# Layer 2 of a graph network stack: context in four 32-column groups, denominators from sums that DMAs accumulate

## The chip, the cores and the metric

The kernel runs on one NeuronCore of a Trainium2 chip. Five engines work side by side, each through its own queue in order: TensorE (PE; its weight loads, PEld, overlap its products), VectorE (DVE), ScalarE (ACT), GpSimd (POOL) and SyncE (SP), which here only issues DMAs. POOL can issue DMAs too. The metric is the device time of one execution in microseconds, as the median of several runs; beside it stands one profiled execution, whose trace gives every instruction's start and length.

## The reference, cut to layer 2

32 graphs of 512 nodes with 256 features go through four layers, each ending in `x = layernorm(x + layer(x, adj))`. Layers 0, 1 and 3 are graph attention, layer 2 is a transformer block with a mask from the adjacency matrix, made symmetric:

```python
eye = jnp.eye(N, dtype=bool)[None]
allowed = (adj > 0) | (jnp.swapaxes(adj, 1, 2) > 0) | eye
qkv = x @ Wqkv.T + bqkv
q, k, v = (heads(t) for t in jnp.split(qkv, 3, axis=-1))   # 8 heads of 32
scores = jnp.einsum('bhqd,bhkd->bhqk', q * scale, k)
scores = jnp.where(allowed[:, None], scores, -jnp.inf)
attn = jax.nn.softmax(scores, axis=-1)
ctx = jnp.einsum('bhqk,bhkd->bhqd', attn, v)
attn_out = ctx.transpose(0, 2, 1, 3).reshape(B, N, DIM) @ Wo.T + bo
x = _layernorm(x + attn_out, ln1_g, ln1_b)
ff = jax.nn.relu(x @ W1.T + b1) @ W2.T + b2
x = _layernorm(x + ff, ln2_g, ln2_b)
```

## The kernel before

Nodes lie on the 128 partitions in R = 4 blocks of rows; features make K = 2 blocks of 128. All products are in float32 (scores in a one-pass form of it), and each float32 product shows as two records in the trace. One graph is a Python generator, `graph(b)`, which yields before each stretch of PE work the time at which that stretch is due: `PERIOD * b + PLACES[stage][i]`. `heapq.merge` over the 32 generators then emits the stretches in the order of these due times, and under `tc.manual_schedule` that is PE's order, fixed. Only the order of the numbers counts, not their size. About four graphs are in work at a time, so between two stretches of one graph's attention stand feed-forward products of the graph before, layer 0 and layer 1 products of the next, and so on. The order on DVE, ACT, POOL and SP is chosen at build time by a scheduler, and is fixed as well; semaphores between the engines are added by the framework. An engine that waits for one instruction holds up all that stand behind it in its queue.

Layer 2, by its functions:

- `qkv` makes queries and keys, splits them into a high and a low part, and lays the parts out by 128 small DMAs of SP a graph; it copies the values into `v` with one extra column of ones per head (width `VC` = 33).
- `attention` goes over four pairs of heads (`hp`). For each of four blocks j of keys it takes two score products into PSUM banks `s`, an exponential on ACT into a tile `pr` of two heads (128x1024, four buffers), and for j < 3 one multiply by the mask on DVE; for j = 3 the mask enters the scores as a second product (`shut`). Then the context, `cp`: for each j and each head of the pair one product whose stationary operand is 64 columns of `v` (the head's 32, its ones column, and columns of the next head that aren't used). The two heads of a pair write the two halves of the partitions of one bank. The ones column makes the softmax denominators as row 32 of each half. A copy on ACT takes the bank to `cs`.
- `attended` turns `cs` back to rows by 16 transposes, takes the reciprocals of the denominators, multiplies, transposes again (8) and multiplies with `wo`.
- `feed_forward` follows, with a `layernorm` at both ends and a further one for the stack. `layernorm` runs statistics on DVE, a power of -1/2 on POOL (the line of `op=ALU.pow`), one small step on DVE, and four normalising activations on ACT. Layer 0 and layer 1 use it too, so POOL does six such powers and one for layer 0's heads in each graph.

PSUM's eight banks are split by stage: two for layers 0 and 1, four for layer 2 up to the projection, two for feed forward and layer 3 (`bank`).

Of the kernel before, what the change touches and what calls it, by code (L numbers as in the profile page):

```python
# [9 lines left out]
F32 = mybir.dt.float32  # L10
# [3 lines left out]
AF = mybir.ActivationFunctionType  # L14
# [12 lines left out]
PERIOD = 12054  # L27
PLACES = {
    "edges": [-1440, -1440, -410, 1420],
    "x": [3260],  # L30
    "mask": [16220, 16520, 16600, 17520],
    "layer 0": [
        2410, 3594, 4534, 4534, 5073, 5753, 5753, 5823, 6123, 6123, 6233, 6233, 6603, 6773, 6903,
        7687, 7687, 7777, 8077, 8077, 8157, 8287, 8439, 8439,
    ],
    "layer 1": [11037, 11066, 11277, 11729, 11849, 11879, 12043, 13286, 13554, 14195, 14884],
    "qkv": [17180, 17740, 18270, 18270, 18270, 18990, 19484, 19654, 21635, 21635],
    "attention": [
        20262, 20932, 21922, 21982, 22092, 22092, 22092, 22350, 22350, 23077, 23537, 23537,
        24028, 24208, 24328, 24532, 25064, 25220, 25368, 25943,  # L40
    ],
    "projection": [26801, 26801, 26861, 26911, 27661, 27721, 28721, 29140, 29256, 29848],
    "feed forward": [
        31013, 31120, 32042, 32263, 32263, 32465, 32710, 33771, 33983, 34076, 34284, 34691,
        35070, 35329, 35615, 36103, 36646, 37299,
    ],
    "layer 3": [39714, 39714, 40906, 41226, 41406, 41526, 41526, 42359, 42359, 42379, 42379],
}
STAGES = {"edges": "a", "x": "a", "layer 0": "a", "layer 1": "a", "feed forward": "c", "layer 3": "c"}
ALL = mybir.DependencyInfo(mybir.DependencyClass.Sync, mybir.DependencyReason.DATA)  # L50


# [20 lines left out]
def fast_path(ctx: ExitStack, tc: tile.TileContext, a: dict, out: bass.AP, bad: bass.AP):  # L73
# [20 lines left out]
    HC = HO + 1  # L94
    VC = DH + 1
    ND = R * (H + 2 + H2)
# [4 lines left out]
    def product(what, *args, **kwargs):  # L101
        latest[0] = what(*args, **kwargs).ins.name  # L102
# [6 lines left out]
    def paced(b, name, units):  # L109

        i = 0
        while True:
            stage[0] = STAGES.get(name, "b")
            try:
                next(units)
            except StopIteration as end:
                return end.value
            yield PERIOD * b + PLACES[name][i]
            i += 1
# [15 lines left out]
    nc.gpsimd.memset(hv, 1.0)  # L135
    v = const.tile([P, R, H2 * VC + 2 * DH - VC], F32, name="v")
    nc.gpsimd.memset(v, 1.0)

# [105 lines left out]
    def buf(shape, tag, name, bufs, dtype=F32):  # L244

        return sb.tile(shape, dtype, tag=tag + stage[0], name=name, bufs=bufs)

    def bank(name, dtype=F32):
        shape = [P, 2048 // (2 if dtype == BF16 else 4)]
        n = 4 if stage[0] == "b" else 2  # L250
        return ps.tile(shape, dtype, tag="mm" + stage[0], name=name, bufs=n)

    def part(name):

        return buf([P, N], "part", name, {"a": 7, "b": 6, "c": 5}[stage[0]])

# [228 lines left out]
    def qkv(x):  # L485
# [31 lines left out]
        for r in range(R):  # L517
            yield
            p = bank("vp")
            for k in range(K):  # L520
                product(nc.tensor.matmul,
                    p[:, :D],
                    xt[:, k, r * P : (r + 1) * P],
                    wqkv[:, k, 2 * D :],
                    start=k == 0,
                    stop=k == K - 1,
                )
            nc.scalar.copy(
                v[:, r, : H2 * VC].rearrange("p (h e) -> p h e", h=H2)[:, :, :DH],
                p[:, :D].rearrange("p (h e) -> p h e", h=H2),  # L530
            )

        return qk

    def attention(qk, a2, shut):
        cs = []
        for hp in range(H2 // 2):
            pr = []
            for j in range(R):
                yield  # L540
                t = sb.tile([P, 2, N], F32, tag="pr", name="pr", bufs=4)
                for i in range(2):
                    s = bank("s")
                    product(nc.tensor.matmul,
                    s,
                        qk[hp][:, 1, i, j * P : (j + 1) * P],
                        qk[hp][:, 0, i, :],
                        start=True,
                        stop=j < R - 1,
                    )  # L550
                    if j == R - 1:
                        product(nc.tensor.matmul, s, identb, shut, start=False, stop=True)
                    nc.scalar.activation(t[:, i, :], s, AF.Exp, scale=QSCALE)  # L553
                if j < R - 1:
                    edges = a2[:, j, :].unsqueeze(1).to_broadcast([P, 2, N])
                    nc.vector.tensor_mul(t, t, edges)  # L556
                pr.append(t)

            yield
            cp = bank("cp")  # L560
            for j in range(R):
                for i in range(2):
                    first = (2 * hp + i) * VC
                    product(nc.tensor.matmul,
                    cp[i * 2 * DH : (i + 1) * 2 * DH, :],
                        v[:, j, first : first + 2 * DH],
                        pr[j][:, i, :],
                        start=j == 0,
                        stop=j == R - 1,
                    )  # L570
            t = part("cs")
            nc.scalar.copy(t, cp)
            cs.append(t)
        return cs

    def attended(x, cs, rd):
        ctx_ = []
        for r in range(R):
            yield
            p = bank("ctp")  # L580
            for hp in range(H2 // 2):
                product(nc.tensor.transpose,
                    p[:, hp * P : (hp + 1) * P], cs[hp][:, r * P : (r + 1) * P], ident
                )
            o = p.rearrange("p (h e) -> p h e", h=H2)
            rdr = rd[:, r * H2 : (r + 1) * H2].unsqueeze(2)
            nc.vector.reciprocal(rdr, o[:, :, DH : DH + 1])
            if r % 2 == 0:
                t = part("ctx").rearrange("p (r d) -> p r d", d=D)
            ctx_.append(t[:, r % 2, :])  # L590
            nc.vector.tensor_mul(
                ctx_[r].rearrange("p (h e) -> p h e", h=H2),
                o[:, :, :DH],
                rdr.to_broadcast([P, H2, DH]),
            )
        ct = yield from transposed(ctx_, "ct")

# [109 lines left out]

    def attended_all(b, x, cs, rd):
        if b == 0:
            weights2()  # L710
        return (yield from attended(x, cs, rd))

# [10 lines left out]
    def graph(b):  # L723
# [11 lines left out]
        qk = yield from paced(b, "qkv", qkv_all(b, x))  # L735
        cs = yield from paced(b, "attention", attention(qk, *a2))
        y = yield from paced(b, "projection", attended_all(b, x, cs, rds[2]))
        x = yield from paced(b, "feed forward", feed_forward_all(b, x, y))
# [662 lines left out]
```

## Time and profile before

| | |
|---|---|
| median of 3 runs | 3910.5 us (3907.77 to 3911.43) |
| span of the profiled execution | 3904.6 us |
| PE, PEld busy | 3753.3, 2824.5 us |
| DVE, ACT, POOL busy | 2674.8, 1926.2, 346.9 us |
| DMA | 261.20 MB, mean 67 GB/s |
| context products `cp`, 2048 records | 474.9 us busy, 600 ns each |
| scores `s`, 1024 records | 395.1 us, 481 ns |
| transposes `ctp` of `cs` and of `ctx`, 512 and 256 records | 67.2 and 39.5 us |

Busy time is the union of an engine's instruction times; overlapping products share it, so 2048 records of 600 ns make 474.9 us of busy time. In a row of the groups stand the line, the engine, the operation, the tiles written and read, the shape, the count, then busy time and mean length of one, then the idle time of the engine in front of it with what ended it. L102 is the line of the helper `product`, through which all matrix products are recorded, so they are told apart by their tiles. `128*64` is the size of the part of the array that a product uses.

### The profile page before, as it was taken

The page shows a single profiled execution, that of the slowest core. Times are in us where ns is not written, and L with a number is a line of the kernel's source. Part 1 is how long each engine was busy: PE and PEld are TensorE (multiplying, and loading weights), DVE is VectorE, ACT ScalarE, POOL GpSimd, SP SyncE. Part 2 cuts the span into 40 slices and gives each one's busy share as a digit, 9 for nine tenths or more (in the row PEclk, how much of TensorE's full clock was granted, in tenths as well). Part 3 has the DMA queues.
Part 4 walks back from the last instruction along what each step waited for, and adds up shares of the span by engine and source line. Part 5 has one row for each costly group of instructions (what it writes and reads, how often), then busy time and mean ns, then how long its engine had stood idle before and what let it go on. Part 6 is the DMA issues. An engine that isn't in the chain of part 4 may idle for free.

```text
span 3904.6 us, 53602 instructions
## 1 busy us (share of the span) xinstructions
PE 3753.3 (96%) x19238; PEld 2824.5 (72%) x19238; DVE 2674.8 (69%) x5594; ACT 1926.2 (49%) x4257; POOL 346.9 (9%) x266
## 2 busy tenths in 40 slices
PE   5899999999999999999999999999999999999996
PEld 4577777777777777777777777777777777777764
DVE  4667676677677677677677677677777677777653
ACT  2444455444455544455544455545555544555442
POOL 0000010000010001010001010001010001010000
PEclk6899999999999999999999999999999999999998
DMA  3222222222222222222222222222222222221120
GB/s 106 77 73 65 72 58 67 71 76 67 70 60 65 71 76 69 68 62 63 71 76 71 66 63 64 69 76 71 66 65 65 65 76 74 63 67 58 49 54 12
DMA packets 180431, 261.20 MB, mean 67 GB/s; under 512 B 36800, under 2 KB 72768, under 8 KB 180160
## 3 DMA queue, kind: packets, MB, share of 16 engines
q1 hardware_dynamic: 180160, 257.71, 23.1%
q8 instruction: 155, 2.54, 0.3%
q14 instruction: 116, 0.95, 0.1%
HBM read 106.57 MB, written 16.78 MB: 32 GB/s over the span
## 4 chain that ended last, share of the span: by engine, by line
PE 60%; DVE 14%; issue 8%; ACT 5%; POOL 5%; POOLq 0%; ACTq 0%
PE o L102 16%; PE f1p L102 7%; PE f2p L102 6%; PE qkp L102 5%; PE cp L102 5%; DVE pr L556 4%; ACT y L275 4%; POOL rs L270 3%; PE h3p L102 3%; PE s L102 3%; PE h1p L102 3%; PE wop L102 3%; POOL st L297 2%; PE gp L102 2%; PE vp L102 2%
## 5 line engine op out<-in xcount | busy, mean ns | idle before, releaser
L556 DVE TENSOR_TENSOR pr<-pr,a 128x1024 f32<-128x1024 f32 x384 | 459.1, 1216 | 319.3 <-ACT pr L553 319.2
L275 ACT ACTIVATE y<-y,rs 128x256 f32<-128x256 f32 x768 | 398.4, 589 | 438.2 <-DVE rs L271 438.2
L393 DVE SCALAR_TENSOR_TENSOR pt<-gb,ex,at 128x512 f32<-128x512 f32 x768 | 530.6, 744 | 77.6 <-ACT gb L345 77.6
L553 ACT ACTIVATE pr<-s 128x512 f32<-128x512 f32 x1024 | 545.2, 613 | 7.4 <-PE s L102 7.3
L102 PEld LDWEIGHTS o<-hv,pt 128*128 128x128 f32 x4096 | 508.4, 199 | 23.7 <-issue 8.4
L102 PE MATMUL o<-hv,pt 128*128 128x65 f32 x4096 | 502.7, 280 | 9.7 <-DVE pt L393 9.7
L102 PE MATMUL f2p<-wf,ft 128*128 128x256 f32 x2048 | 491.6, 383 | 12.3 <-ACT ft L638 12.2
L102 PE MATMUL cp<-pr,v 128*64 128x512 f32 x2048 | 474.9, 600 | 17.8 <-DVE pr L556 17.1
L102 PE MATMUL f1p<-yt,wf 128*128 128x256 f32 x2048 | 488.9, 381 | 0.3 <-DVE yt L302 0.3
L102 PE MATMUL o<-h,pt 128*128 128x257 f32 x2048 | 482.8, 383 | 3.7 <-DVE pt L393 3.7
L102 PEld LDWEIGHTS o<-h,pt 128*128 128x128 f32 x2048 | 381.5, 190 | 96.0 <-issue 40.6
L270 POOL TENSOR_TENSOR rs<-rs,mhalf 128x4 f32<-128x4 f32 x192 | 246.2, 1282 | 2118.8 <-DVE rs L269 1826.0
L638 ACT ACTIVATE ft<-f1p,cols 128x256 f32<-128x256 f32 x512 | 215.2, 474 | 442.2 <-PE f1p L102 442.2
L102 PEld LDWEIGHTS f2p<-wf,ft 128*128 128x128 f32 x2048 | 380.1, 191 | 69.5 <-ACT ft L638 17.1
L102 PEld LDWEIGHTS f1p<-yt,wf 128*128 128x128 f32 x2048 | 385.3, 191 | 54.5 <-DVE yt L302 0.8
L102 PE MATMUL s<-qk 128*128 128x512 f32 x1024 | 395.1, 481 | 1.6 <-ACT pr L553 1.6
L102 PEld LDWEIGHTS cp<-pr,v 128*64 128x64 f32 x2048 | 133.0, 136 | 286.0 <-issue 194.2
L266 DVE BATCH_NORM_STATS2 bn<-y 128x6 f32<-128x256 f32 x768 | 294.6, 411 | 4.5
L102 PEld LDWEIGHTS s<-qk 128*128 128x128 f32 x1024 | 187.8, 190 | 99.3 <-issue 40.6
L102 PE MATMUL qkp<-xt,wqkv 128*128 128x512 f32 x512 | 231.3, 594 | 0.0
L345 ACT COPY gb<-gp 128x512 f32<-128x512 f32 x192 | 111.5, 581 | 219.4 <-PE gp L102 219.4
L428 DVE RECIPROCAL rd<-o 128x4 f32<-128x4 f32 x128 | 23.4, 183 | 272.7 <-PE o L102 272.7
(134 smaller groups left out, 4582.5 us busy)
## 6 DMA issues: line engine op xcount, KB each, us to landing
qk<-hi SPq DMA_DIRECT2D x1024, 64.0 KB, 2.0
qk<-lo SPq DMA_DIRECT2D x1024, 64.0 KB, 2.0
adjt<-in_adjt SPq DMA_DIRECT2D x64, 512.0 KB, 3.5
adj<-in_adj SPq DMA_DIRECT2D x64, 512.0 KB, 3.6
xt<-in_xt SPq DMA_DIRECT2D x32, 512.0 KB, 3.4
x<-in_x SPq DMA_DIRECT2D x32, 512.0 KB, 4.7
out<-y SPq DMA_DIRECT2D x32, 512.0 KB, 3.0
wf<-in_w1t SPq DMA_DIRECT2D x1, 1024.0 KB, 7.6
```

The source lines that it names most:

```text
L102: latest[0] = what(*args, **kwargs).ins.name
L266: nc.vector.bn_stats(st[:, r, :], y[:, r, :])
L270: nc.gpsimd.tensor_tensor(rs[:, 1, :], rs[:, 0, :], mhalf[:, :R], op=ALU.pow)
L275: nc.scalar.activation(y[:, r, :], y[:, r, :], AF.Identity, bias=rs[:, 2, r : r + 1], scale=rs[:, 1, r : r + 1],)
L297: nc.gpsimd.tensor_tensor(st[:, 2, :], st[:, 1, :], mhalf[:, :G], op=ALU.pow)
L345: nc.scalar.copy(g, p)
L393: nc.vector.scalar_tensor_tensor(t, g, f, edges, op0=ALU.max, op1=ALU.mult)
L428: nc.vector.reciprocal(rdh, o[:, :, HO:])
L553: nc.scalar.activation(t[:, i, :], s, AF.Exp, scale=QSCALE)
L556: nc.vector.tensor_mul(t, t, edges)
L638: nc.scalar.activation(ft[:, f, :], p[:, f, :], AF.Relu, bias=bf1[:, ff + f : ff + f + 1])
```

## The change

Context: the loop now goes over the two column blocks c of the context. Four heads share one bank, each with its 32 columns of `v` (no ones column any more), so the four products of a block of keys write four groups of 32 partitions. The scores of two head pairs alternate, j by j; the context products come in two blocks per c, after j = 1 and after j = 3. `cp` lies the right way round already: a copy takes it into `ct`.

Denominators: the tiles of j = 1, 2, 3 are added onto that of j = 0 by DMAs that accumulate, issued from POOL, three for each of the four head pairs, twelve a graph. After the attention the sums `totals` are multiplied by a tile of ones in eight products (`den`, four groups of 32 partitions), copied, transposed by four products, inverted, spread over 32 columns by an ACT copy, transposed back by eight products, and multiplied into `ct`.

Buffers: `pr` has seven in place of four; PSUM is one set of eight banks for all stages; the space kept for descriptors of POOL's DMAs is 8192 in place of the default. `PERIOD` is the same, all numbers in `PLACES` are new, so PE's order is new everywhere.

```diff
-    v = const.tile([P, R, H2 * VC + 2 * DH - VC], F32, name="v")
+    v = const.tile([P, R, D], F32, name="v")
+    ones = const.tile([P, K, DH], F32, name="ones")
+    nc.gpsimd.memset(ones, 0.0)
+    for c in range(K):
+        nc.gpsimd.memset(ones[:, c, c : c + 1], 1.0)
...
-        n = 4 if stage[0] == "b" else 2
-        return ps.tile(shape, dtype, tag="mm" + stage[0], name=name, bufs=n)
+        return ps.tile(shape, dtype, tag="mm", name=name, bufs=8)
...
     def attention(qk, a2, shut):
+        ct = buf([P, K, N], "ct", "ct", 1)
+        totals = []
+        for c in range(K):
+            cp = bank("cp")
+            pr = []
             for j in range(R):
+                pr.append([])
+                for hp in range(2):
+                    yield
+                    t = sb.tile([P, 2, N], F32, tag="pr", name="pr", bufs=7)
...
+                    pr[j].append(t)
+                if j % 2 == 0:
+                    continue
                 yield
+                for jj in (j - 1, j):
+                    for hh in range(4):
+                        product(nc.tensor.matmul,
+                        cp[hh * DH : (hh + 1) * DH, :],
+                            v[:, jj, (4 * c + hh) * DH : (4 * c + hh + 1) * DH],
+                            pr[jj][hh // 2][:, hh % 2, :],
+                            start=jj == 0,
+                            stop=jj == R - 1,
+                        )
+                for hp in range(2):
+                    for jj in (j - 1, j):
+                        if jj:
+                            add_to(pr[0][hp], pr[jj][hp])
+            nc.scalar.copy(ct[:, c, :], cp)
+            totals.append(pr[0])
+        return ct, totals
+
+    def add_to(t, u):
+        nc.gpsimd.dma_start(t, u, accum_op=ALU.add)
+
+    def attended(x, ct, totals, rd):
+        yield
+        den = bank("den")
+        for c in range(K):
+            for hh in range(4):
+                product(nc.tensor.matmul,
+                    den[hh * DH : (hh + 1) * DH, :],
+                    ones[:, c, :],
+                    totals[c][hh // 2][:, hh % 2, :],
+                    start=c == 0,
+                    stop=c == K - 1,
+                )
+        dens = buf([P, N], "dens", "dens", 1)
+        nc.scalar.copy(dens, den)
+        yield
+        dt = bank("dt")
+        for r in range(R):
+            product(nc.tensor.transpose,
+                dt[:, r * P : (r + 1) * P], dens[:, r * P : (r + 1) * P], ident
+            )
+        rdc = rd.rearrange("p (c r h) -> p c r h", c=K, r=R)
+        nc.vector.reciprocal(
+            rdc,
+            dt.rearrange("p (r h e) -> p e r h", r=R, h=4)[:, :K],
+        )
+        for c in range(K):
+            rdb = buf([P, R, 4, DH], "rdb", "rdb", 1)
+            nc.scalar.copy(rdb, rdc[:, c].unsqueeze(3).to_broadcast([P, R, 4, DH]))
+            rdbs = rdb.rearrange("p r h e -> p r (h e)")
             yield
+            g = bank("rdp")
+            for r in range(R):
                 product(nc.tensor.transpose,
+                    g[:, r * P : (r + 1) * P],
+                    rdbs[:, r, :],
+                    ident,
+                )
+            nc.vector.tensor_mul(ct[:, c, :], ct[:, c, :], g)
...
-    nc = bacc.Bacc("TRN2", target_bir_lowering=False, num_devices=1)
+    nc = bacc.Bacc("TRN2", target_bir_lowering=False, num_devices=1, dynamic_dma_scratch_size=8192)
```

In the built program the tile of the last two heads of j = 3 takes the buffer of an earlier tile of the same group (j = 2), which must first have been read by the context products and added by its DMA. For c = 1 PE's order is, in 29 of the 32 graphs: context block (8 products), 4 scores, 4 f2p, 2 h0p, 4 o1, 4 scores with mask, 4 o1, context block, 4 o1, 8 den, 4 dt, 4 o1, 2 h0p, 4 rdp, 8 xt3p, 4 rdp.

112 lines of the change are left out of this document (34 added, 78 removed).

## The prediction

> **What bounds the kernel now.** I read engine shares first, then the pace of one graph, then the windows.
>
> ```profile
> PE 3753.3 (96%) x19238; PEld 2824.5 (72%) x19238; DVE 2674.8 (69%) x5594; ACT 1926.2 (49%) x4257; POOL 346.9 (9%) x266
> ```
>
> From the timeline of PE, the same block of layer 0 in two neighbouring graphs:
>
> ```profile
> 1515.47 3.68 PE L102 MATMUL o<-hv,pt 128*128 128x65 f32 x32
> ...
> 1632.24 3.68 PE L102 MATMUL o<-hv,pt 128*128 128x65 f32 x32
> ```
>
> So a graph takes 116.77 us in the steady state, and 31 of these leave 285 us for filling and draining. The windows view (window, its length, then PE, PEld, DVE, ACT, POOL busy; granted clock after them) says how full PE is, and what a pause costs:
>
> ```profile
> 2400.00:2520.00 120.00, 118.31 (x617) 89.72 (x616) 84.55 (x176) 62.45 (x139) 10.76 (x8) 1.00 0.23 66
> ...
> 267.20:270.60 3.40, 0.09 (x1) 0.00 (x0) 1.67 (x4) 2.02 (x5) 1.15 (x1) 1.00 0.44 110
> 270.70:274.00 3.30, 2.93 (x7) 2.40 (x8) 1.22 (x1) 3.07 (x6) 0.00 (x0) 0.50 0.24 60
> ```
>
> PE is idle 1.7 us of 120 in the steady state: it sets the pace, and matmul time taken out is worth its full length, unless PE must wait instead. After the one pause of 3.77 us at 267 the next 3.4 us were granted half the clock: a long pause is paid for again, by about 1.7 us.
>
> **What the products cost.** Timeline of PE, eight transposes and a context block of 16 records (eight pairs in two groups of 64 columns), each with what follows it:
>
> ```profile
> 1681.98 1.09 PE L102 MATMUL xt1p<-ident,y 128*128 128x128 f32 x8
> 1682.91 1.89 PE L102 MATMUL f2p<-wf,ft 128*128 128x256 f32 x8
> ...
> 1694.43 3.65 PE L102 MATMUL cp<-pr,v 128*64 128x512 f32 x16
> 1698.02 0.73 PE L102 MATMUL s<-qk 128*128 128x512 f32 x2
> ```
>
> A product in float32 is two records. Eight pairs take 3.59 us to the next product: 0.43 us a pair, with 0.1 us lost where the tile shape changes. Both groups of a pair thus go at the pace of one. Transposes cost 0.93/8 = 0.116 us.
>
> **The change, part by part, for one graph.**
>
> Context: 64 records as 32 pairs, 13.8 us. After, they are 16 fours; if four groups go together as two do, 6.9 us: −6.9. The trace has no four groups: bounds 6.9 (all together) and 13.8 (two at a time); I take 6.9, since the pair shows no price at all. [...]
>
> Removed besides: 16 + 8 transposes (ctp), 2.8 us. Added: denominators, eight products as four fours, 1.7 us; 4 + 8 transposes, 1.4 us; one more change of shape, 0.1. Together −6.9 − 2.8 + 3.2 = **−6.4 us of PE** a graph. If nothing else happened: 32 × 6.4 = 205 us off.
>
> DVE loses four reciprocals, four multiplies and a copy (0.18, 0.42, 0.66 us each: 3.1 us) and gains one reciprocal and two 128x512 multiplies (1.6); ACT loses five 0.58 us copies and gains five. Neither binds: no gain, no cost. One set of eight banks in place of 2 + 4 + 2: nothing, as long as ACT empties the score banks in time. Gone from SP: nothing. The smaller descriptor space: nothing.
>
> **The new waits.** Twelve accumulating DMAs of 512 KB a graph go out on POOL. In the built order they chain: each waits on POOL for the landing of the one before it on the same sum, and behind them on POOL stand the layernorms' power operations, for which DVE waits in place, and ACT behind DVE. The seven pr buffers add to it: an exponential waits on ACT until an add has landed and released its buffer. The rows, from the page and from the groups of 1220 to 2196 us:
>
> ```profile
> L270 POOL TENSOR_TENSOR rs<-rs,mhalf 128x4 f32<-128x4 f32 x192 | 246.2, 1282 | 2118.8 <-DVE rs L269 1826.0
> L275 ACT ACTIVATE y<-y,rs 128x256 f32<-128x256 f32 x768 | 398.4, 589 | 438.2 <-DVE rs L271 438.2
> L553 ACT ACTIVATE pr<-s 128x512 f32<-128x512 f32 x1024 | 545.2, 613 | 7.4 <-PE s L102 7.3
> L556 DVE TENSOR_TENSOR pr<-pr,a 128x1024 f32<-128x1024 f32 x384 | 459.1, 1216 | 319.3 <-ACT pr L553 319.2
> ...
> L476 ACT ACTIVATE relu<-o,rd 128x256 f32<-128x256 f32 x36 | 16.7, 463 | 34.7 <-DVE rd L475 34.7
> L480 DVE SCALAR_TENSOR_TENSOR y<-relu,y 128x512 f32<-128x512 f32 x18 | 12.2, 677 | 0.0
> L654 DVE TENSOR_TENSOR y<-y,ln2g_b 128x1024 f32<-128x1024 f32 x9 | 11.0, 1225 | 18.6 <-ACT y L275 18.6
> ```
>
> No accumulating DMA is in the trace. Let X be one, from issue to landing. Nearest rows:
>
> ```profile
> q1 hardware_dynamic: 180160, 257.71, 23.1%
> ...
> qk<-hi SPq DMA_DIRECT2D x1024, 64.0 KB, 2.0
> out<-y SPq DMA_DIRECT2D x32, 512.0 KB, 3.0
> ```
>
> Below: 3.0 us, as a plain store of the same size. 257.71 MB took 23.1% of 16 × 3904.6 us, so 512 KB hold all sixteen engines 1.83 us. An add must read the sum as well: 3.0 + 1.83 = 4.8, and 6.7 where it shares the engines with its neighbour, the upper end. I take 4.8. [...]
>
> Now the tightest stretch, the second column group (c = 1), in the order that 29 of 32 graphs share. Between its first context block and the middle of its second PE has, counted in records: block 1.72, four scores 1.2, eight f2p 1.73, four h0p 0.89, eight o1 1.75, four scores with mask 2.24, eight o1 1.75, half a block 0.86, shape changes 0.4: 12.5 us. The chain beside it: the block's first products end (1.03), add lands (X), two exponentials in the buffer it frees (1.23), mask (1.22), statistics and reciprocal on DVE (1.06), power (1.28), DVE (0.16), four layernorm activations (2.36), Relu and Exp (0.93), the last two exponentials (1.23), eight hand-overs of 0.07 (the context's end to its copy on ACT): 11.1 + X. PE waits X − 1.4 = 3.4 us. Next late: the last add starts only then and the denominators need it; X less half a block, o1 and half the denominators (3.5) is 1.3 us of waiting. Next: denominators to their transposes, with nothing between them on PE: end and hand-overs 0.31, copy 0.58, 0.9 us. Sum: 2X − 4.0 = **5.6 us**. Were the adds free, PE would wait still: from the first o1's end on come the reciprocal 0.15, small DVE steps 0.5, power 1.28, four activations 2.36, on DVE two of 1.22, two of 0.68 and four statistics with their aggregates 2.1, then reciprocal, Relu and Exp 1.1, the denominators' copy 0.58 and hand-overs 0.7, 12.6 us in all, beside 2.24 + 1.75 + 1.72 + 1.75 + 1.72 = 9.2 of PE: never under 3.4. At X = 6.7: 9.4. The first column group has 15 us more of PE behind it; there I cost the waits at nothing, which holds up to X of about 7.
>
> A pause of 3.4 us brings the half clock: +1.7 us, from 0 (the slow stretch hides behind the last add) to 3.4 (two such windows).
>
> **Sum**: −6.4 + 5.6 + 1.7 = +0.9 us a graph, +29 us in 32. The profiled execution, 3904.6 us, becomes 3934; the runs' median lies 5.9 above their profile: **3940 us**. Ends: −6.4 + 3.4 + 0 = −3.0 (3815); −6.4 + 9.4 + 1.7 = +4.7 (4060).
>
> **The rivals.**
>
> *PE's gain shows* (0.31). X near 3.5, the floor 3.4 to 4.5 stands, clock stays full: −2 to −3 us a graph, 3815 to 3850. For it: DMA engines are 23% busy and plain 512 KB take 3.0; against it: the sum is read again, and the pause at 267 did cost the clock.
>
> *Adds far slower* (0.15). X of 6.7 or more at the shared engines; each us costs 2 a graph: 4060 and up. For it: two adds go out together each time; against: twelve adds of 3.7 us of engine time are 44 of 117 us.
>
> *No fourfold context* (0.07). Fours run as pairs: 6.9 + 1.7 us back, part of it under the waits: about +6 a graph, 4130. For it: only pairs were ever seen; against: their 0.43.
>
> *Forecast* (0.47): the waits eat the products' gain, slightly slower. The four share the place where it is decided: break-even is at X = 4.35 with the half clock, 5.2 without it.
>
> Range for 8 in 10: 3825 to 4065; the forecast's own 3915 to 3985. A difference under 0.2% (8 us) can't be told from none. Faster: that first rival and 0.03 of the forecast, 0.34; same: 0.08 of the forecast; slower: the rest of it (0.36) and the other two, 0.58.
>
> **What would show it.** Right: cp records in fours 0.43 us apart; period near 117.7; PE idle before the second context block's last products, before den and before dt; granted clock at 0.5 once a graph; pr exponentials and DMAs waiting for adds. Wrong: X under 4, a period near 114, clock at 1.00 throughout.

## The result, and the profile after

| | before | after |
|---|---|---|
| median of four runs, us | 3909.4 (3907.8 to 3911.4) | 4222.1 (4217.3 to 4227.2) |
| span of the profiled execution, us | 3904.6 | 4219.1 |
| one graph in the steady state, us | 116.77 | 126.16 |
| of it, PE idle | 1.68 | 11.83 |
| of it, lost to the half clock | 0 | 3.7 |

The ratio is 1.080, 95% interval 1.0784 to 1.0815: slower, as forecast in sign, but by 313 us and not by 30, and outside the range. A graph is the mean distance between the starts of its second transposes (xt2p) over the middle twenty graphs. The idle time comes from the window from 1000 to 3000 us, scaled to one graph; the clock's share is half of PE's busy time in the half-clock stretches there. (Half of their whole length, the measure that the prediction and the expectations use, is 5.1, but 1.4 of that is idle time already counted.)

The shares, the granted clock and the DMA share by slices of the span, from the page of the changed kernel:

```profile
PE 3735.8 (89%) x19302; PEld 2792.3 (66%) x19366; DVE 2638.6 (63%) x5402; ACT 1946.8 (46%) x4257; POOL 683.2 (16%) x652
...
PEclk7799999999999999999999999999999999999998
DMA  3544555544555544455544455544455544455450
```

PE is busy only 17.5 us less than before, although its products need some 200 us less: the half clock and the draining around each wait stretch what is left. Next the groups, the queues and the DMA issues of the same page:

```profile
q0 software_dynamic: 55296, 201.35, 26.0%
q1 hardware_dynamic: 180160, 257.71, 21.6%
...
L100 PE MATMUL s<-qk 128*128 128x512 f32 x1024 | 409.0, 503 | 204.8 <-DMA qk<-lo 204.8
...
L580 POOL DMA_DIRECT2D pr<-pr x384 | 338.5, 910 | 837.8 <-DVE mv L267 164.4
...
L100 PE MATMUL cp<-pr,v 128*32 128x512 f32 x2048 | 344.6, 612 | 105.3 <-ACT pr L554 67.7
...
pr<-pr POOLq DMA_DIRECT2D x384, 512.0 KB, 5.7
```

The adds land in 5.7 us at the median (4.8 was forecast). But the largest wait is none that the forecast named: the scores wait for the copies qk<-lo. PE's waits between 1000 and 3000 us (us in all, times, longest) say how it divides; 16 graphs fit in there:

```profile
PE s L100 <- DMA qk<-lo: 100.8, 32, 5.7
PE cp L100 <- ACT pr L554: 34.9, 16, 3.3
PE f2p L100 <- ACT ft L661: 24.2, 16, 1.5
PE cp L100 <- DVE pr L557: 12.0, 16, 0.8
PE dt L100 <- ACT dens L595: 11.1, 16, 0.7
PE den L100 <- DMA pr<-pr: 4.6, 5, 1.8
```

So 6.3 us a graph are lost at the second column group's first scores, and 5.5 at five smaller places. In these rows f1p and f2p are the two feed-forward products, with the activation ft between them; vp are the values' products, xt1p and h1p layer 1's transposes and products, which need layer 0's norm. One graph on PE's timeline (start, length, tile, records, and in brackets the idle time before them):

```profile
2049.28 1.91 PE L100 MATMUL cp<-pr,v 128*32 128x512 f32 x12
2051.95 1.05 PE L100 MATMUL cp<-pr,v 128*32 128x512 f32 x4 [0.75 <-DVE pr L557]
2052.93 1.20 PE L100 MATMUL s<-qk 128*128 128x512 f32 x4
...
2059.36 1.92 PE L100 MATMUL cp<-pr,v 128*32 128x512 f32 x16
2061.22 1.99 PE L100 MATMUL f1p<-yt,wf 128*128 128x256 f32 x8
...
2067.84 1.91 PE L100 MATMUL h1p<-w1g,xt 128*128 128x258 f32 x8
2075.31 0.76 PE L100 MATMUL s<-qk 128*128 128x512 f32 x1 [5.57 <-DMA qk<-lo]
2076.71 0.80 PE L100 MATMUL s<-qk 128*128 128x512 f32 x1 [0.63 <-DMA qk<-lo]
2077.30 3.62 PE L100 MATMUL f2p<-wf,ft 128*128 128x256 f32 x8
...
2096.72 1.91 PE L100 MATMUL cp<-pr,v 128*32 128x512 f32 x12
2100.32 1.53 PE L100 MATMUL cp<-pr,v 128*32 128x512 f32 x4 [1.69 <-ACT pr L554]
...
2106.39 1.05 PE L100 MATMUL den<-pr,ones 128*32 128x512 f32 x4 [0.76 <-DMA pr<-pr]
2108.12 0.66 PE L100 MATMUL dt<-ident,dens 128*128 128x128 f32 x4 [0.69 <-ACT dens L595]
```

Three things are to be seen. An undisturbed context block takes 1.86 us to the next product (2059.36 to 2061.22), where it took 3.59: the fours go together at 0.43 us each, as forecast. The stall at the scores is followed by f2p at twice its length: 3.62 us against 1.89. And a wait costs more than its bracket: the block at 2049.28 takes 3.65 us to the next product, 1.79 more than the undisturbed one, for 0.75 us shown: the twelve records ahead of the wait show as 1.91 us, as long as the sixteen of the undisturbed block, and the four behind it as 1.05. I call this draining and refilling; the profile counts it as busy. The windows (length, PE, PEld, DVE, ACT and POOL busy, granted clock, DMA share, GB/s) give the clock of the stretch behind the stall:

```profile
1000.00:3000.00 2000.00, 1812.38 (x9510) 1360.97 (x9541) 1289.29 (x2641) 962.88 (x2106) 339.06 (x319) 0.96 0.50 113
2074.10:2080.90 6.80, 4.96 (x11) 3.68 (x12) 1.22 (x1) 3.19 (x5) 0.00 (x0) 0.51 0.38 114
```

The books for one graph: −6.4 of products, +10.15 idle, +3.7 of clock make +7.45 of the measured +9.39. The 1.9 left over is not measured by itself; I put it down to draining and refilling beyond what the brackets show. 31 graphs make 291 of the 314 us between the profiled spans; the other 23 lie at both ends. That the first and last graphs have nothing to cover the adds is the likely reason (e3 and e14 below, without adds, do not have these 23).

### The profile page after: what moved, and what is told of

Read it like the earlier page. It is cut to its first block, busy times and chain, and to the rows that moved or that the text cites. A ratio compares the mean times of both kernels' runs of the same rounds, so it can differ in the third digit from the quotient of the medians.

```text
span 4219.1 us, 54746 instructions
## 1 busy us (share of the span) xinstructions
PE 3735.8 (89%) x19302; PEld 2792.3 (66%) x19366; DVE 2638.6 (63%) x5402; ACT 1946.8 (46%) x4257; POOL 683.2 (16%) x652
## 3 DMA queue, kind: packets, MB, share of 16 engines
q1 hardware_dynamic: 180160, 257.71, 21.6%
## 4 chain that ended last, share of the span: by engine, by line
PE 62%; DVE 9%; SPq 8%; DMA 7%; issue 6%; ACT 5%; POOL 3%; POOLq 0%; ACTq 0%; DVEq 0%
PE o L100 20%; SPq L512 8%; PE f1p L100 7%; PE f2p L100 6%; DMA pr<-pr 5%; PE qkp L100 5%; DVE pr L557 4%; PE s L100 3%; PE cp L100 3%; PE h3p L100 3%; PE vp L100 3%; PE wop L100 2%; PE h0p L100 2%; POOL st L297 2%; PE gp L100 2%
## 5 line engine op out<-in xcount | busy, mean ns | idle before, releaser
L100 PE MATMUL s<-qk 128*128 128x512 f32 x1024 | 409.0, 503 | 204.8 <-DMA qk<-lo 204.8
L100 PE MATMUL f2p<-wf,ft 128*128 128x256 f32 x2048 | 541.8, 412 | 54.2 <-ACT ft L661 53.9
L100 PE MATMUL o<-h,pt 128*128 128x257 f32 x2048 | 503.1, 391 | 2.3 <-DVE pt L393 2.3
L100 PEld LDWEIGHTS f2p<-wf,ft 128*128 128x128 f32 x2048 | 414.5, 208 | 132.9 <-ACT ft L661 71.8
L580 POOL DMA_DIRECT2D pr<-pr x384 | 338.5, 910 | 837.8 <-DVE mv L267 164.4
L270 POOL TENSOR_TENSOR rs<-rs,mhalf 128x4 f32<-128x4 f32 x192 | 232.4, 1210 | 1274.0 <-DVE rs L269 1250.6
L100 PE MATMUL cp<-pr,v 128*32 128x512 f32 x2048 | 344.6, 612 | 105.3 <-ACT pr L554 67.7
L100 PEld LDWEIGHTS s<-qk 128*128 128x128 f32 x1024 | 202.3, 203 | 313.6 <-issue 228.1
L297 POOL TENSOR_TENSOR st<-st,mhalf 128x16 f32<-128x16 f32 x32 | 120.0, 3751 | 935.3 <-DVE st L296 935.3
L100 PEld LDWEIGHTS cp<-pr,v 128*32 128x32 f32 x2048 | 67.3, 109 | 293.7 <-ACT pr L554 123.2
```

Of the source, the lines that this page charges most:

```text
L270: nc.gpsimd.tensor_tensor(rs[:, 1, :], rs[:, 0, :], mhalf[:, :R], op=ALU.pow)
L297: nc.gpsimd.tensor_tensor(st[:, 2, :], st[:, 1, :], mhalf[:, :G], op=ALU.pow)
L580: nc.gpsimd.dma_start(t, u, accum_op=ALU.add)
```

## Why the scores wait

Behind the scores' copies stands SP's queue. Its own waits (DMA queue's line, what it waited for: us in all, times, longest) and its timeline in the graph just shown, for the changed kernel:

```profile
SPq L711 <- DVE bn L266: 463.1, 28, 16.8
...
SPq L512 <- PE s L100: 79.8, 31, 18.5
...
2037.61 1.23 SPq L512 DMA_DIRECT2D qk<-lo  x2
2054.79 0.37 SPq L711 DMA_DIRECT2D x<-in_x  x1
2056.57 0.51 SPq L512 DMA_DIRECT2D qk<-hi  x1
...
2070.67 3.30 SPq L512 DMA_DIRECT2D qk<-hi  x2
2074.01 1.22 SPq L512 DMA_DIRECT2D qk<-lo  x2
```

The sixteen copies into the fourth qk tile (c = 1, heads 6 and 7) start only at 2056.57 and take 18.7 us, 1.17 us apiece, where SP otherwise issues one in 0.63. Two causes for the start are in sight. The rows' load x<-in_x stands ahead of them in SP's order (before it stood behind all of a graph's copies) and waits 16 us for DVE. And qk has three buffers for four tiles: the fourth takes the first one's, which is read until the first group's last scores, since the head pairs now alternate key block by key block. For the pace, the last four adds of the first group (issued from 2058.0 to 2069.2 us) run beside them: the page counts both queues on sixteen engines, 26.0% of their time for the adds and 21.6% for the rest.

## The experiments

All ratios are to the kernel before, run beside them on the same chip, with the 95% interval.

**Who holds the copies: the load, the adds, or both.** Four runs together. The first, e1:

```diff
-        nc.sync.dma_start(x, a["x"][b].rearrange("(r p) d -> p r d", p=P))
+        in_place(nc.sync.dma_start(x, a["x"][b].rearrange("(r p) d -> p r d", p=P)))
```

> The changed kernel, with one line altered: the load of the next graph's rows (x<-in_x on SP) is tied to the place on TensorE at which it is written, so that on SP it stands behind the last sixteen qk copies of the second column group and not ahead of them; orders of PE, ACT and POOL stay. Theory Q (the load waits on SP for layer 0's end, 16 us, with the sixteen copies behind it): the scores' waits for qk<-lo, 6.3 us a graph, are gone, the half-clock window of about 7 us behind them (worth 3.4) too, so 8 to 9.5 us a graph less: 3920 to 3965 us. Theory C (the copies are late because the accumulating DMAs take their DMA engines; the place in the queue is not what matters): the scores still wait 4 us or more a graph, 4150 us or more. Theory S (the stall of 2X - 4 at the second context block carries the loss): within 1% of 4222.

4226.1 us, ratio 1.081 (1.079 to 1.082): nothing gained, theory Q as it was put is wrong. SP's waits and timeline of this run name the other holder:

```profile
SPq L512 <- PE s L100: 551.6, 32, 18.5
...
2044.96 1.22 SPq L512 DMA_DIRECT2D qk<-lo  x2
2063.46 0.51 SPq L512 DMA_DIRECT2D qk<-hi  x1
...
2080.78 1.22 SPq L512 DMA_DIRECT2D qk<-lo  x2
```

With the load out of the way SP waits for PE's scores, 17.2 us a graph against 2.6: the fourth tile's buffer, freed at the first group's masked scores (2062.4 to 2064.2 us here). In the changed kernel the load's wait ended 1.8 us before that and hid it. The copies still take 18.5 us. Then e2, without the adds:

```diff
-                for hp in range(2):
-                    for jj in (j - 1, j):
-                        if jj:
-                            add_to(pr[0][hp], pr[jj][hp])
...
-        nc.scalar.copy(dens, den)
+        nc.scalar.activation(dens, den, AF.Copy, bias=1.0)
```

> The changed kernel without its twelve accumulating DMAs a graph; the denominators are then the first key block's sums plus 1, so three of four key blocks' sums are left out. The rows' load stays ahead of the sixteen qk copies on SP. If the load's place alone makes the scores late (Q alone): the 16 us wait on SP stays, waits for qk<-lo of 3 us a graph or more, 4000 us or more. If it takes both, the load's wait and copies that the adds stretch from 0.6 to 1.16 us each (Q with C): the copies end 8 us earlier, the waits for qk<-lo fall under 0.5 us a graph, and 3800 to 3900 us. PE's other idle time (at the second context block, den and dt) goes from 3.1 us a graph to between 1 and 3.

4022.9 us, ratio 1.029 (1.028 to 1.031). No scores wait for copies any more, but the time is 120 us above the most that the joint theory gave. PE waits 3.0 us a graph at dt: on ACT four norm activations that are not ready now stand ahead of the denominators' copy, and half clock follows (granted clock 0.98 from 1000 to 3000 us, 1.00 in the kernel before). The order on ACT changed with the edit, so this run can't price the load's place.

And e3, without the adds and with the load behind:

> Both edits at once: no accumulating DMAs (three of four key blocks' sums are left out of the denominators) and the rows' load behind the copies. Every theory: no scores wait for qk copies. By the prediction's PE sum (-6.4 us a graph) with a floor of 0 to 3.4 us of waits a graph: 3705 to 3815 us. If it lies at 3815 to 3900, there is a loss that neither the adds nor the queue's place explains (the half clock, or the places of PE's units).

3894.9 us, ratio 0.996 (0.995 to 0.998), clock at 1.00 from 1000 to 3000 us. SP's timeline, the first and the last of the sixteen copies:

```profile
2024.02 0.51 SPq L512 DMA_DIRECT2D qk<-hi  x1
...
2032.80 1.22 SPq L512 DMA_DIRECT2D qk<-lo  x2
```

The copies start when the buffer comes free, as in the first run, but take 10.0 us (2024.02 to 2034.02), and no score waits. So the adds stretch the copies, and without them the late buffer alone does no harm. But the time lies at the upper end: even with no adds only 0.4 us a graph are won where the prediction's sum had 3.0. That is taken up below. In e4, with e1's edit kept, GpSimd adds by itself:

```diff
-        nc.gpsimd.dma_start(t, u, accum_op=ALU.add)
+        nc.gpsimd.tensor_add(t, t, u)
```

> The rows' load behind the copies, and the twelve sums a graph made by GpSimd itself (tensor_add of 128x1024 in place) and not by accumulating DMAs. The DMA engines go back to a busy share near 0.24. If an add on POOL takes up to 2 us (24 us a graph of POOL), it is at least as good as the first of these runs: 3850 to 3960 us. If it takes 4 us or more, or slows DVE beside it, the sums come later than by DMA (5.7 us) only in their chain: 4000 us or more, with PE waiting before den.

4519.7 us, ratio 1.156 (1.154 to 1.158). The sums are whole here and no DMA adds: the sixteen copies take 11.0 us and again no score waits for them, which bears e3 out. But an add on GpSimd takes 2.5 us at the median, and DVE is slower beside it: its masks take 1.39 us on average against 1.22, the pt products 0.90 against 0.74. The medians stay at 1.22 and 0.74, so some are held up (34 of 384 masks take over 1.3 us, up to 3.4) and most not at all.

**One buffer more.** The test of both causes together, with the adds kept (e5):

```diff
-            t = [sb.tile([P, 2, 2, N], F32R, tag="qk", name="qk", bufs=3) for _ in range(2)]
+            t = [sb.tile([P, 2, 2, N], F32R, tag="qk", name="qk", bufs=4) for _ in range(2)]
...
-            rdb = buf([P, R, 4, DH], "rdb", "rdb", 1)
+            rdb = buf([P, N], "dens", "rdb", 1).rearrange("p (r h e) -> p r h e", r=R, h=4)
...
-    nc = bacc.Bacc("TRN2", target_bir_lowering=False, num_devices=1, dynamic_dma_scratch_size=8192)
+    nc = bacc.Bacc("TRN2", target_bir_lowering=False, num_devices=1, dynamic_dma_scratch_size=2048)
```

> The changed kernel with four qk buffers in place of three (8 KB found by a descriptor space of 2 KB in place of 8 and one buffer for dens and rdb); the adds stay. The sixteen copies into the fourth qk tile then need not wait for PE to have read the first, and in the built order the rows' load stands behind them. Theory K (the scores of the second column group are late because of two things together: the fourth tile's buffer comes free only at the first group's last scores, and then the adds stretch its sixteen copies from 0.6 to 1.16 us each): the waits for qk<-lo, 6.3 us a graph, fall under 0.5, most of the half clock (5.1 us a graph) goes with them; 3930 to 4010 us (8 to 9.5 us a graph less than 4222, or 6.5 if the waits at cp, den and dt keep some half clock). Theory C (the adds' traffic alone makes the copies late, wherever they stand): 4150 us or more.

3929.3 us, ratio 1.005 (1.003 to 1.007): 293 us come back, which puts the time at the lower end of what theory K said. The waits for qk<-lo are gone, PE idles 5.4 us a graph, half clock costs 0.8 (granted clock 0.99 from 1000 to 3000 us), a graph takes 116.87 us; all of a graph's copies are out 1 us before the first group's adds begin, and an add lands in 5.2 us at the median. In this build the rows' load also stands behind the copies (the last copies go out at 2031.90, the load at 2041.97), so both holders are gone. e1 shows that the load's place alone gains nothing; four buffers with the load still ahead were not run. The control, e6, has the last two edits without the buffer:

> Control for the run beside it: the changed kernel with the descriptor space of 2 KB and the shared buffer for dens and rdb alone, every engine's order as in the changed kernel. If these two do nothing by themselves: 4205 to 4240 us and adds that still take 0.9 us to issue and 5.7 us to land. If the small descriptor space holds POOL back, the adds' issue grows and the time with it.

One run, 4220.6 us, adds at 0.90 and 5.7 us: they do nothing by themselves.

**Where the products' 6.4 us are.** What is left is a kernel with 6.4 us less for PE in each graph that takes as long as before: 3.7 more idle and 0.8 of half clock take 4.5 of it, and 2.0 are left over, as 1.9 were in the changed kernel. PE's waits in e5 are short (a graph: f2p 1.5, cp 0.8 and 2.2, dt 0.7, den 0.2 us), so the next runs cover them by other places. All keep the four buffers. First e7:

```diff
     "feed forward": [
-        31005, 31424, 32055, 32120, 32459, 33080, 33486, 33900, 34009, 34404, 34544, 34982,
+        31005, 31424, 32055, 32120, 32459, 33080, 33225, 33900, 34009, 34404, 34544, 34982,
...
     "attention": [
-        19907, 20239, 21375, 21375, 22352, 22373, 22393, 22796, 22796, 23073, 23567, 23991,
+        21192.5, 21192.5, 21192.5, 21192.5, 22000, 22000, 22352, 22373, 22393, 22796, 22796, 23073, 23567, 23991,
...
+                for r in range(R // 2, R) if c + j == 1 else ():
+                    yield
+                    p = bank("vp")
```

> The run with four qk buffers, with other places in the first column group: f1p one unit earlier, ahead of layer 0's last products, then the first group's eight scores, and the last two vp units (moved into attention) between f1p and the f2p that waits 1.5 us for ft in every graph. If PE's pauses there (f2p 1.5 us, cp 0.76 us and 0.3 to 0.5 us of refilling behind each) are lost time and nothing else is behind them: 2 to 3 us a graph less than 3929, 3835 to 3870 us. If ACT, which must do the scores' exponentials meanwhile, is what ends them, they move to the context block: 3900 to 3940 us.

4166.2 us, ratio 1.066 (1.065 to 1.068). The waits at f2p and the first cp are gone, and a new one of 8 us stands at xt1p, for layer 0's norm, with half clock behind it (mean granted clock of the execution 0.942, 0.974 in e5). In e9 the second group's waits are covered:

```diff
-        24234, 24375, 24502, 24962, 25104, 25791, 26007, 26278, 26278,
+        24234, 24375, 24502, 24962, 25104, 25791, 26007, 26310, 26310,
...
-    "projection": [26574, 26779, 27626, 28093, 29538, 29538, 30404, 30404, 30473],
+    "projection": [26900, 27300, 28095, 28780, 29538, 29538, 30404, 30404, 30473],
```

> The run with four qk buffers, with other places in the second column group: one layer 1 unit ahead of the last context block and not behind it, the next ahead of den, an h0p unit between den and dt, and the rdp units later. If the pauses there (cp 1.8, den 0.2, dt 0.7 us and their refilling) only lack work to cover them: 2 us a graph less than 3929, 3850 to 3880 us. If the last exponentials are held by the layer 1 statistics and activations that precede them on ACT and DVE, the order there moves with PE's and the wait stays: 3910 to 3940 us.

3921.5 us, ratio 1.003 (1.002 to 1.004): 0.3 us a graph, with the half clock gone (granted clock 1.00 from 1000 to 3000 us), and not 2 us. The wait at cp falls from 2.2 to 0.4 us a graph, but dt's grows to 1.0 and rdp gets one of 0.8. Both edits make e8:

> The edit of e7_fill_f2p and that of e9_fill_den together. If the waits are PE's alone and independent: 4 to 5 us a graph less than 3929, 3770 to 3815 us. If PE's waits in the second group go back to the chain of adds and layernorms (the prediction's floor of 3.4 us), they reappear before den or dt: 3830 to 3880 us.

4149.0 us, ratio 1.062 (1.060 to 1.064): e7's wait at xt1p decides.

Three milder fills of the first group, on top of e9: e10 and e11 move two vp units or one between f1p and the f2p that waits (as in e7, with the first four entries of "attention" at 21550 and layer 0 left alone), e12 the third key block's scores ahead of the first context block:

```diff
-        19907, 20239, 21375, 21375, 22352, 22373, 22393, 22796, 22796, 23073, 23567, 23991,
+        19907, 20239, 21375, 21375, 21990, 21990, 22352, 22796, 22796, 23073, 23567, 23991,
...
-                if j % 2 == 0:
+                now = {(0, 2): (0, 1), (0, 3): (2, 3), (1, 1): (0, 1), (1, 3): (2, 3)}.get((c, j))
+                if not now:
```

> The run e9_fill_den with one more move: the last two vp units go between f1p and the f2p that waits for ft, so the first group's eight scores come one f1p's length (1.78 us) earlier; unlike e7_fill_f2p nothing of layer 0 is moved on PE. If layer 0's norm was late in e7 because its last products were put back on PE: xt1p does not wait, f2p's wait of 1.5 us and its refilling go, 3850 to 3880 us. If it was late because the scores' exponentials and masks stand ahead of the norm on ACT and DVE: xt1p waits 2 us or more, 3920 us or more.

> As e10_vp_gap, with one vp unit moved and the scores 0.89 us earlier. f2p's wait falls from 1.5 to about 0.6 us; the same two cases, half their size: 3885 to 3905 us, or xt1p waits and 3920 us or more.

> The run e9_fill_den with the third key block's scores of the first group (four records, 1.04 us) between f1p and the f2p that waits, ahead of the first context block; the scores before them stay where they are. f2p's wait falls from 1.5 to 0.5 us and cp's of 0.76 to 0.3: 3870 to 3900 us. If the pr buffers (six of seven are then written before a context block frees any) or ACT hold it back: the wait moves to cp or to the masked scores, 3915 us or more.

3931.5, 3922.2 and 3919.8 us, ratios 1.006 (1.004 to 1.008), 1.003 (1.002 to 1.005) and 1.003 (1.002 to 1.004). In e10 and e11 f2p waits 0 and 0.65 us and cp takes it over (2.1 and 1.25 us for DVE's mask); xt1p doesn't wait. In e12 f2p's wait falls to 0.6 and cp keeps its 0.8; xt1p begins to wait (0.2 us). None gains on e9 beyond the intervals.

Two runs on e9 asked what sets the pace instead, e13 by taking masks out:

```diff
-                    if j < R - 1:
+                    if j == 0:
                         edges = a2[:, j, :].unsqueeze(1).to_broadcast([P, 2, N])
```

> The run e9_fill_den without the multiplications by the edges for the key blocks 1 and 2 (that part of the mask is left out): eight DVE instructions of 1.22 us a graph less, 9.7 us of DVE, and not one product less on PE. Theory L (with PE's 6.4 us out, the pace is set by the dependent steps on ACT and DVE between PE's units, in one order for all graphs, so that filling one wait opens another; e9 to e12 all stayed at 116.5 to 117.0 us a graph): the period falls by 1.5 us or more though PE has the same work: 115 us or less a graph, 3870 us or less. Theory W (the waits left on PE are separate ones that the moves failed to fill): PE's work is the same and its waits outside cp stay: 116 us or more, 3905 to 3925 us.

4041.9 us, ratio 1.034 (1.032 to 1.036): slower with less work. On ACT an ft activation now stands behind a norm's four activations that wait for DVE, f2p waits up to 3.4 us and half clock follows (granted clock 0.98 from 1000 to 3000 us). As a test of L it failed, since ACT's order moved. One thing can be read: layer 0's statistics are ready 18.4 us after its last products, against 22.1 in e9. And e14, e9 without the adds (edit as in e2):

> The run e9_fill_den without the accumulating DMAs (three of four key blocks' sums are left out of the denominators). What the adds still cost once the qk copies are out of their way: by the prediction 2X - 4.0 - 3.4 = 4 us a graph at the measured X of 5.7, so about 3795 us; by theory L next to nothing in the steady state (PE waits 0.3 us a graph for them at den) and 10 to 20 us at both ends together: 3895 to 3915 us.

3914.7 us, ratio 1.001 (1.000 to 1.002); the steady graph takes 117.2 us, 0.6 more than with the adds. In the steady state nothing is gained by leaving the adds out once the copies are out of their way. What the adds alone cost is not isolated by this: the wait at cp grows from 0.4 to 1.6 us a graph, since ACT's order moved here too (shown for e3 below). e14 is 7 us faster only at the ends, which take 278 us of its profiled span and 306 of e9's.

Then the last wait of the first group was covered, on top of e12, by moving the first context block behind the next f1p (22352 becomes 22500), e15:

> The run e12_scores_gap with the first context block one f1p unit later, so that the wait for DVE's mask (0.76 us shown, some 1.8 us with its draining and refilling) is covered. If the waits on PE are separate: 1.5 to 1.8 us a graph less than 3920, 3862 to 3875 us, faster than the kernel before. If the third and fourth blocks' exponentials, which need buffers that this block and its adds free, come later by as much: the wait moves to the second context block and 3910 to 3930 us.

4044.1 us, ratio 1.035 (1.033 to 1.037). cp doesn't wait for the mask; xt1p waits for the norm, 3.1 us a graph. In e16 xt1p comes later (xt1p and h1p at 11613 and 12050, one pair of scores at 23668):

> The run e15_cp_later with layer 1's first transposes (xt1p, which waited 3.2 us a graph for layer 0's norm) behind the next f2p and f1p units, 3.5 us later on PE, and h1p behind them. If the wait at xt1p was the only thing that e15's move brought up: the half clock goes too and 3850 to 3880 us, faster than the kernel before. If f2p, whose ft stands on ACT behind that norm, takes the wait over: 3990 us or more, and the norm's end, not PE's order, is what this stretch hangs on.

4079.9 us, ratio 1.043 (1.042 to 1.045): f2p takes the wait over, some 5 us a graph, since its ft stands behind the norm on ACT. So the wait hangs on the norm's end, not on PE's order. The last edit takes work off DVE there, in e12 (e17) and in e15 (e18):

```diff
-        nc.vector.tensor_add(y, x, all_rows(bo))
-        nc.vector.tensor_add(x, x, all_rows(ln2b))
+        in_place(nc.vector.tensor_add(y, x, all_rows(bo)))
+        in_place(nc.vector.tensor_add(x, x, all_rows(ln2b)))
```

> The run e12_scores_gap with two additions of 1.2 us (bo and ln2b, in attended) held on DVE until PE has come to the rdp units, so that they leave the stretch between layer 0's last product and its norm, where DVE is busy 23.8 of 25.5 us. Theory V (DVE sets the length of that stretch, so PE's waits there can't be filled): the norm ends 1.2 us or more earlier after the last product (25.5 us before), the waits at f2p (0.6) and cp (0.8) stay, being ahead of the norm, and the time changes little unless xt1p (0.2) or what follows it waited: 3900 to 3925 us. Theory W (waits on PE alone): the norm's end stays within 0.5 us.

> The run e15_cp_later (4044 us, xt1p waiting 3.2 us a graph and some half clock behind it) with the same two additions held back. Theory V: DVE has 1.2 to 2.4 us less to do before the norm, so xt1p's wait falls from 3.2 to 0.8 to 2.0 us and the half clock (2.5 us a graph) goes: 3870 to 3960 us. Theory W: within 1% of 4044.

3915.0 us, ratio 1.002 (1.001 to 1.002), and 3892.7 us, ratio 0.996 (0.995 to 0.997). e18 computes everything and beats both kernels, by 0.4% and 7.8%; its steady graph takes 115.8 us. But theory V is the smaller part of it. DVE's and POOL's timelines of e15 (L269 has the statistics ready, L270 is the power on POOL, L271 what DVE makes of it, L581 an add):

```profile
2099.48 0.15 DVE L269 SCALAR_TENSOR_TENSOR rs<-mv 128x4 f32<-128x4 f32 x1
...
2103.80 0.16 DVE L271 SCALAR_TENSOR_TENSOR rs<-mv,rs 128x4 f32<-128x4 f32 x1 [2.31 <-POOL rs L270]
...
2097.64 0.86 POOL L581 DMA_DIRECT2D pr<-pr  x1 [3.56 <-DVE bn L266]
2101.82 0.89 POOL L581 DMA_DIRECT2D pr<-pr  x1 [3.32 <-DVE y L624]
2102.39 1.38 POOL L270 TENSOR_TENSOR rs<-rs,mhalf 128x4 f32<-128x4 f32 x1
```

and of e18:

```profile
2020.59 0.15 DVE L269 SCALAR_TENSOR_TENSOR rs<-mv 128x4 f32<-128x4 f32 x1
...
2021.89 0.16 DVE L271 SCALAR_TENSOR_TENSOR rs<-mv,rs 128x4 f32<-128x4 f32 x1 [0.60 <-POOL rs L270]
...
2019.51 0.86 POOL L581 DMA_DIRECT2D pr<-pr  x1 [3.58 <-DVE bn L266]
2020.83 1.03 POOL L270 TENSOR_TENSOR rs<-rs,mhalf 128x4 f32<-128x4 f32 x1 [0.45 <-DVE rs L269]
2023.67 0.94 POOL L581 DMA_DIRECT2D pr<-pr  x1 [1.81 <-ACT y L275]
```

In e15 the power stands on POOL behind an add that goes out 4.2 us after the add before it (by the program it waits for an earlier one on its own sum to land; its bracket names DVE); in e18 it stands ahead of that add. Measured from layer 0's last products, the statistics are ready after 22.9 and 22.2 us, and L271 is done after 27.2 and 23.5: 0.7 us of the 3.8 is DVE's, the rest is the turn on POOL. In e12 and e17 no power is held so, and L271 is done only 0.2 us earlier (24.2 and 24.1).

## Why the prediction was wrong, step by step

**The step that failed** is "Gone from SP: nothing", and beside it "The first column group has 15 us more of PE behind it; there I cost the waits at nothing". On SP nothing was taken out, but what its queue waits for was moved: the first qk tile is read until the group's end, and the fourth tile's sixteen copies wait for it. That the buffer was tight could be read in the kernel before, in SP's waits:

```profile
SPq L512 <- PE s L102: 310.6, 32, 11.1
```

9.7 us a graph, covered there because the first pair ends two whole pairs before the fourth begins. With the adds beside them the copies then ran at little more than half their pace (1.17 us apiece, 0.63 in e3) into the scores, which wait 6.3 us a graph for them. e1 shows the buffer, e3 and e4 the adds, and e5 that the time comes back when neither the buffer nor the load holds the copies: 293 of the 313 us.

**The half clock** was put at 1.7 us a graph by half the stretches' length; by that measure it came to 5.1 (3.7 of PE's busy time), most of it behind that unforeseen stall. In e5 it is 0.8.

**The products** were right: fours at 0.43 us, 1.86 us a block. In the changed kernel's trace the sixteen records of a block in four column groups go in 1.86 us, where eight undivided ones of the same 512 columns (qkp at 2007.31) take 3.43, 0.43 us each: four went in about the time of one.

**X** was right in size: 5.2 us at the median in e5, 5.7 in the changed kernel, for 4.8. What it was built from, that reading the sum costs as much again as a plain transfer (1.83 us of the engines' time, so 3.7 an add), was an estimate; an add's engine time came to 2.9 us.

**The stall of 2X − 4.0** was too large. At X = 5.7 it would be 7.4 us; the brackets at the last context block, den and dt make 3.2. Without adds (e3) they make 1.5, so the adds lengthen this place by about 1.7 us, and the floor ("never under 3.4") shows as 1.5 of idle time there. In e3 and e14 that gain is lost again elsewhere: the first group's second context block waits 1.6 us, which it does not in e5 or e9. ACT's timeline of e3 shows why:

```profile
2027.76 2.08 ACT L275 ACTIVATE y<-y,rs 128x256 f32<-128x256 f32 x4 [1.09 <-DVE rs L271]
2029.74 0.57 ACT L554 ACTIVATE pr<-s 128x512 f32<-128x512 f32 x1
```

The block's last exponential has come to stand behind layer 0's norm; in e5 all four stand ahead of it. So in e3 the −3.0 of the sum came out as −0.4: of the products' 6.4 us, 3.7 went into more idle time than before, 1.6 of it at this block, and 2.4 are left over.

**What waits cost beyond their length** has no term in the sum. If the remainders above are this, it is 1.9 to 2.4 us a graph, 60 us or more in 32; it is read directly only at single waits.

**"Neither binds: no gain, no cost"**, said of DVE and ACT from their shares, did not hold in one stretch. From layer 0's last products to its statistics it takes 21.7 us before, 22.1 in the changed kernel and in e3, e5, e9 and e14. The windows view of e5 from there on, and the one long wait of DVE in it:

```profile
2020.58:2046.08 25.50, 23.24 (x115) 15.43 (x115) 21.49 (x35) 15.92 (x34) 8.37 (x6) 1.00 0.60 144
...
2033.24 1.22 DVE L298 TENSOR_TENSOR y<-y,st 128x1024 f32<-128x1024 f32 x1 [2.79 <-POOL st L297]
```

DVE is busy 21.5 of the 25.5 us (the 23.8 in the expectation of e17 adds up lengths that overlap), and most of the rest is a wait for a step on POOL. In the kernel before, PE filled the way to xt1p, 27.1 us, with less than 1 us between the norm's end and xt1p. Products moved into or out of it (e7, e10, e11, e16) give waits in place of time. That this stretch sets the pace is argued from these runs; none isolates it.

**The mechanism on POOL** that the text described, a norm's power behind a waiting add, is real: 3 us in e15, and about as much in e7 and e16. In the changed kernel itself the power is not held (0.2 us at 2059.08).

**Of the rivals**, "adds far slower" ended in the region of the result (4060 and up) by another way: the median of X never reached 6.7, though 80 of the changed kernel's 384 adds took longer. The forecast's own sum, 3940, is what the kernel takes with the one buffer more, 3929; but that agreement is partly luck, since 2X − 4.0 stood in for waits at other places, drains and refills. What is still open is whether the rest of the 6.4 us can be had: e18 has 0.9 of it, with 3.8 us of PE idle a graph left, most of it at dt, rdp, cp, f2p and den.

## What to carry to other kernels

When the order in which tiles are read is changed, list for each rotating buffer which queue waits for its release and what is queued behind; the queue's own waits in the kernel before show which of them are already tight. Judge whether an engine binds by the stretch, not by its share of the span: DVE's 69% of the span in the kernel before is 21.9 of the 26.1 us from layer 0's last products to the norm's end. And read the order on every in-order queue again after each edit: here runs with work taken out (e2, e13) lost 120 us to a copy or an activation that had come to stand behind a norm, and in e3 and e14 an exponential behind a norm hid what the adds cost.

## What was not expected of the hardware

- A wait of PE within a context block cost about 1 us more than the idle time shown: 1.79 us for 0.75 in the changed kernel, 2.68 for 1.65 in e3. At f2p it was less: 1.9 for 1.5.
- An accumulating DMA of 512 KB took 2.9 us of all sixteen engines' time (26.0% of 16 × 4219.1 us for 384 of them), against 1.83 us for 512 KB of plain copies (23.1% of 16 × 3904.6 us for 257.71 MB in the kernel before); and beside these adds SP needed nearly twice the time for each small copy, 1.17 us against 0.63 (e3).
- Waits up to 1.7 us came without half clock in the steady state of e3, e9, e11, e12, e14, e17 and e18 (mean granted clock of the whole execution 0.978 to 0.981). With a wait of 2.1 us in each graph (e10) half clock came in 4 of 17 graphs (mean 0.976), with waits of 2.2 us on average and up to 3.3 (e5) in 7 of 17 (0.974), and where a wait of some 3 us stood in each graph (e2, e13, e15) in each (0.964 to 0.965).
- Beside GpSimd's adds DVE's instructions were longer on average, the masks 1.39 us for 1.22 and the pt products 0.90 for 0.74, with the medians unchanged (e4).
